# Ones in the graph table's rows, and residuals added by ScalarE and TensorE in the second attention layer of a four-layer graph network

## The chip, the core and the metric

The kernel runs on one core of a Trainium2 chip. The metric is the device time of one execution in microseconds (us): before the change 3109.28 us, the median of four runs that lie between 3100.89 and 3118.96 us. Engines are named as in the profile: PE (TensorE matmuls), PEld (TensorE weight loads), DVE (VectorE), ACT (ScalarE), POOL (GpSimd), SP (SyncE, which here only starts transfers).

## What is computed

Eight batches of 2048 nodes with 128 features pass through four layers on one sparse adjacency matrix. Layers 0 and 2 are attention layers, layers 1 and 3 are graph-attention layers ("graph layers" below). Per batch:

```python
# layers 0 and 2
scores = einsum('bnhd,bmhd->bhnm', x @ Wq, x @ Wk) / sqrt(16), masked by adj     # 8 heads of 16
x = layer_norm(x + (softmax(scores) @ (x @ Wv)) @ Wo + bo) * ln1_g + ln1_b
x = layer_norm(x + relu(x @ W1 + b1) @ W2 + b2) * ln2_g + ln2_b                  # W1: 128x256
# layers 1 and 3
h = x @ W;  e = leaky_relu((h @ a_src)[:, None] + (h @ a_dst)[None, :]), masked by adj
x = layer_norm(x + softmax(e) @ h) * ln_gamma + ln_beta
```

Each node has about 17 neighbours, so the kernel works on lists of neighbours, not on the whole matrix. If a list does not fit, a second, dense program (class `Dense`) runs instead; the given input does not need it.

## The kernel before, in words

**Units and tiles.** The 2048 nodes are cut into 32 units of 64 nodes. A unit holds its nodes for two halves of the batch (4 batches each), so a tile `[128, 512]` is 4 batches of 128 features. The neighbours of a unit are gathered in 9 slots of 128 rows: four pairs and a single one, which makes five steps `t` per unit.

**Tables.** Each layer reads a table in HBM with one row per node. An attention row holds keys and values of all 8 batches, 8 x 256 floats = 8192 bytes. A graph row holds, per batch, the 128 centred features of `h` and one float, the score `h @ a_dst`: 8 x 129 floats = 4128 bytes. `project` (L1290) makes the rows of the next layer from a finished unit (matmul with `Wkv` or `Wx`, copy to `trows`, store L1354 by SP). A layer's gathers (`gather`, L1410, issued by POOL at L1422) wait until the whole table is stored, so between layers the pipeline runs empty and fills again.

**An attention unit** (`attention`, L1437). Queries are made by PE (L1456) and copied by ACT (L1460). Per step: POOL gathers a pair of slots into one of six `kv` buffers; PE spreads the queries over the slots into the four PSUM banks of `qe` (L1495); DVE multiplies keys by them (L1507) and sums over 16 features (L1514); ACT takes the exponent (L1524); POOL, or for some tiles DVE, multiplies values by it (L1533); PE adds the slots up into `acc` and `sums` (L1561), which frees the buffer.

`after_attention` (L1575) then finishes the unit: DVE inverts the sums and divides (L1579 to L1586); PE transposes, ACT copies to `at` (L1606); PE multiplies by `Wo` as one 128x512 matmul into `ps_o` (L1282); DVE adds bias and residual into `r` (`add_to`, L1598); PE multiplies `r` by a constant matrix (identity minus 1/128), which transposes it back and takes the mean away (`centred`, L1272); ACT squares, takes the root and scales (`norm`, L1369 to L1391); PE transposes, ACT applies gain and offset (`scaled`, L1408). Then `W1` with relu (L1282, L1617), `W2` into `ps_y` (L1629), and `add_to`, `centred`, `norm`, `scaled` once more.

**A graph unit** (`graph`, L1649). Per step DVE adds the two scores and applies the leaky slope (L1735, L1742), ACT takes the exponent (L1747), DVE spreads it over a one-hot matrix into `w` (L1757), and PE adds the weighted rows up (L1784): 16 matmuls with 32 columns of weights and 128 features each, all into one PSUM bank, which a matmul with zeros has cleared (L1701). Four more small matmuls per step sum the weights themselves into `sums` (L1795). `after_graph` (L1806) inverts the sums (L1814), scales (L1822), and goes on as above.

**What sets the order.** All operations are recorded first, each with its engine, a cost in microseconds, a key (due time), and the buffers that it takes. `Plan.order` runs a list scheduler over them: on each engine the ready operation with the smallest key goes first, if its buffers are free. The resulting order is fixed in the program, and each engine works through its own list strictly in that order. A changed cost or a changed operation can therefore move operations on all engines, in other layers too. [...]

Of the kernel before, what the change touches and what calls it, by code (L numbers as in the profile page):

```python
# [9 lines left out]
F32 = mybir.dt.float32  # L10
# [730 lines left out]
class Sparse:  # L741
# [15 lines left out]
    def __init__(self, ctx, tc, x, xt, adj, w, out):  # L757
# [16 lines left out]
        for tag, bufs in PSUM_BUFS.items():  # L774
# [14 lines left out]
            self.dram.tile([self.N, self.B * (2 * P if kind is MHA else P + 1)], F32, name=f"table_{n}")  # L789
# [141 lines left out]
    def mha_weights(self, n):  # L931
        const, w = self.const, self.w[n]
        d = {}
        for name, shape in (("Wq", [P, P]), ("Wkv", [P, 2 * P]), ("Wo", [P, P]), ("W1", [P, FFN])):
            if n or name != "Wkv":
                d[name] = const.tile(shape, F32, name=f"{name}_{n}")
        d["W2"] = const.tile([P, FFN // P, P], F32, name=f"W2_{n}")
        if n:
            self.fill(n, (d["Wkv"][:, 0:P], w["Wk"]), (d["Wkv"][:, P : 2 * P], w["Wv"]))
        else:  # L940
            d["Wkv"] = self.layers[0]["Wkv"]
        self.fill(
            n,
            (d["Wq"], w["Wq"]),
            (d["Wo"], w["Wo"]),
            (d["W1"], w["W1"]),
            (d["W2"], w["W2"].rearrange("(c p) m -> p c m", p=P)),
        )
        d["b1"] = self.column(n, "b1", FFN // P)
        for name in ("bo", "ln1_g", "ln1_b", "b2", "ln2_g", "ln2_b"):  # L950
            d[name] = self.column(n, name)
        return d

    def gat_weights(self, n):
# [7 lines left out]
            (wx[:, 0:P], w["W"]),  # L962
# [7 lines left out]
        op({"PE": 0.3}, lambda e: e.transpose(ps.tile[:, 0:P], wx[:, 0:P], self.ident), key, reads=[at], writes=[ps])  # L970
# [10 lines left out]
        def centre(e):  # L981
            e.tensor_copy(wx[:, P : P + 2], ps2.tile[:, 0:2])
            e.tensor_reduce(mean, wx[:, 0:P], axis=mybir.AxisListType.X, op=ALU.add)
            e.tensor_scalar(mean, mean, 1.0 / P, None, ALU.mult)
            e.tensor_scalar(wx[:, 0:P], wx[:, 0:P], mean, None, ALU.subtract)
# [290 lines left out]

    def product(self, w, x, key, name, out):
# [12 lines left out]
    def project(self, n, u, x, key, of=None, shares=()):  # L1290
# [4 lines left out]
        width = 2 * P if mha else P + 1  # L1295
        rows = self.cell(("trows", "hidden", "trows")[u % 3] if n == 0 else "trows", [P, hb * width], name="trows")
        for v in range(2):
# [29 lines left out]
            else:  # L1327

                self.op(
                    {"ACT": 0.48},  # L1330
                    lambda e, ps=ps, v=v: e.copy(
                        rows.tile.rearrange("p (b d) -> p b d", b=hb)[:, 2 * v : 2 * v + 2, :],
                        ps.tile[:, :, 0 : P + 1],
                    ),
# [68 lines left out]
    def scaled(self, rows, gamma, beta, tag, key):  # L1403
# [8 lines left out]
        )  # L1412
        return x
# [158 lines left out]
    def after_attention(self, n, u, acc, sums, x, base):  # L1572
# [34 lines left out]
        r = cell("r", [P, CH], name="r1")  # L1607
        ps = self.product(L["Wo"], at, key, "ps_o", r)
        add_to(r, ps, L["bo"], x, key - 2)
        normed = self.norm(self.centred(r, key), key)  # L1610
        x1 = self.scaled(normed, L["ln1_g"], L["ln1_b"], "x1", key)
# [12 lines left out]
        r = cell("r", [P, CH], name="r2")  # L1624
        ps = cell("m", [P, CH], name="ps_y")
        for f in range(FFN // P):
            op(
                {"PE": 1.0},
                lambda e, f=f, ps=ps: e.matmul(  # L1629
                    ps.tile,  # L1630
                    lhsT=L["W2"][:, f, :],
                    rhs=hidden.tile[:, f, :],
                    start=(f == 0),
                    stop=(f == FFN // P - 1),
                ),
                key,
                reads=[hidden],
                writes=[ps],
                holds=[r],
            )  # L1640
        add_to(r, ps, L["b2"], x1, key - 2)
        normed = self.norm(self.centred(r, key), key)
# [6 lines left out]
    def graph(self, n):  # L1649
        hb = self.HB  # L1650
        width = hb * (P + 1)
        op, cell = self.op, self.cell
        for u in range(self.NU):
# [36 lines left out]
            if u % 2:  # L1690
                both = cell("q", [P, 4, CH], name="acc_q")
                outs = [both]
                acc, sums = (lambda both=both: both.tile[:, 0, :]), (lambda both=both: both.tile[:, 1, 0:hb])
            else:
                outs = [cell("acc", [P, CH]), cell("sums", [P, hb])]
                acc, sums = (lambda outs=outs: outs[0].tile), (lambda outs=outs: outs[1].tile)

            def clear(e, acc=acc):
                for s in range(P // GROUP):
                    rows = slice(s * GROUP, (s + 1) * GROUP)  # L1700
                    e.matmul(  # L1701
                        acc()[rows, :],
                        lhsT=self.zeros[:, 0:GROUP],
                        rhs=self.zeros,
                        start=True,
                        stop=False,
                    )


            op({"PE": 0.3}, clear, base, reads=[te, self.table[n]], writes=outs)  # L1710
# [3 lines left out]
            for i, t in enumerate(steps):  # L1714
# [15 lines left out]
                def both_rows(kv, at=at, tiles=tiles):  # L1730
                    rows = kv.tile[:, at % 4 * 2 * width : (at % 4 + tiles) * 2 * width]
                    return rows.rearrange("p (j b d) -> p j b d", j=tiles, d=P + 1)

                def score(e, t=t, kv=kv, te=te, e8=e8, both_rows=both_rows, tiles=tiles):
# [3 lines left out]
                        both_rows(kv)[:, :, :, P].rearrange("p j (h b) -> p j h b", h=2),  # L1738
# [27 lines left out]
                def add(  # L1766
                    e,
                    t=t,
                    kv=kv,
                    hot=hot,  # L1770
                    e8=e8,
                    w=w,
                    acc=acc,
                    sums=sums,
                    both_rows=both_rows,
                    tiles=tiles,
                    first=i == 0,
                    last=i == TG - 1,
                ):
                    for b in range(hb):  # L1780
                        for j in range(2):
                            for hf in range(2):
                                rows = slice((2 * hf + j) * GROUP, (2 * hf + j + 1) * GROUP)
                                e.matmul(  # L1784
                                    acc()[rows, b * P : (b + 1) * P],
                                    lhsT=w.tile[:, j, hf * hb + b, :],
                                    rhs=both_rows(kv)[:, j % tiles, hf * hb + b, 0:P],
                                    start=False,
                                    stop=(last and b == hb - 1),
                                )  # L1790
                    for j in range(2):
                        for hf in range(2):
                            rows = slice((2 * hf + j) * GROUP, (2 * hf + j + 1) * GROUP)
                            col = GS + (j * TG + t) * GROUP
                            e.matmul(  # L1795
                                sums()[rows, :],
                                lhsT=hot.tile[:, col : col + GROUP],
                                rhs=e8.tile[:, j % tiles, hf * hb : (hf + 1) * hb],
                                start=first,
                                stop=last,  # L1800
                            )

                op({"PE": 1.8}, add, key, reads=[now, hot, e8, w], writes=outs, shares=[kv])
            self.after_graph(n, u, outs, acc, sums, x, base)

    def after_graph(self, n, u, outs, acc, sums, x, base):  # L1806
# [6 lines left out]
        def inverse(e):  # L1813
            e.tensor_scalar(rc.tile, sums(), 1e-30, None, ALU.max)  # L1814
            e.reciprocal(rc.tile, rc.tile)

        op({"DVE": 0.35}, inverse, base, reads=outs, writes=[rc])
        a = cell("rows", [P, hb, P], name="a")
        for b in range(hb):
# [3 lines left out]
                    a.tile[:, b, :], acc()[:, b * P : (b + 1) * P], AF.Copy, scale=rc.tile[:, b : b + 1]  # L1823
# [137 lines left out]
```

## Time and profile before

| | us |
|---|---|
| median of four runs | 3109.28 (3100.89 to 3118.96) |
| the execution that was profiled | 3117.2 |
| span of its profile | 3115.2 |
| layer 0, attention, with the building of the lists | about 0 to 1160 |
| layer 1, graph | about 1200 to 1660 |
| layer 2, attention | about 1670 to 2640 |
| layer 3, graph | about 2643 to 3115 |

Busy time in the span: PE 2435.7 us (78%), PEld 1495.3 (48%), DVE 2210.2 (71%), ACT 1382.4 (44%), POOL 2132.2 (68%). The transfers moved 1087.97 MB.

How to read it. In a group's row stand line, engine, operation, out<-in, the count, then busy time and mean length of one instruction (ns), then the idle time of that engine just before them and what ended it. A matmul of 32-bit floats is two instructions in these counts. In a list of waits, "DVE r L1598 <- PE ps_o L1282" means that DVE stood idle until that PE instruction was done. A table of windows gives for each stretch the busy time and count of PE, PEld, DVE, ACT and POOL, then the granted clock of PE (1.00 is full), the mean busy share of the 16 DMA engines (packets overlap a little, so it can pass 1.00) and the rate. PE's busy time counts pipelined matmuls in full, so the distance from one start to the next tells more. A line of the timeline is start, length, engine, line, operation.

### The profile page before, as it was taken

Reading aid. Unit: us, or ns where it says so; the run is one execution under the profiler, and the core shown is the slowest. Engines: PE = TensorE matmul, PEld = TensorE weight load, DVE = VectorE, ACT = ScalarE, POOL = GpSimd, SP = SyncE. Lnnn points to the kernel's source line nnn. Section 1 sums busy time; section 2 is a strip of 40 time slices with the busy share of each in tenths; the row PEclk is TensorE's granted clock in tenths of the full one; section 3 lists DMA queues with packets and bytes.
Section 4 is the critical chain, followed back from the end, with each engine's and each line's share of the span. In section 5 each row is a group of like instructions: output and inputs, shape, how many; then the busy total and the mean of one; then the engine's idle time right before and its main releaser. Section 6 shows DMA issues by size and latency. Waiting matters only on the chain.

```text
span 3115.2 us, 68763 instructions
## 1 busy us (share of the span) xinstructions
PE 2435.7 (78%) x26280; PEld 1495.3 (48%) x26280; DVE 2210.2 (71%) x3420; ACT 1382.4 (44%) x4749; POOL 2132.2 (68%) x1461
## 2 busy tenths in 40 slices
PE   7878887778877776878887678888888887777775
PEld 5634444344333334767765234333334343666765
DVE  4879998889887772444443888988899894555554
ACT  4535545445544443444444144444444444343433
POOL 1168877768888874656653788888788883766663
PEclk8679989989999997888888799999999998787787
DMA  8889989889998976999997999999899994999996
GB/s 282 291 310 368 370 318 367 318 304 371 363 364 321 356 274 231 411 405 403 398 401 280 369 365 370 369 380 378 342 366 384 375 379 147 388 407 400 400 404 242
DMA packets 270865, 1087.97 MB, mean 349 GB/s; under 512 B 41216, under 2 KB 59904, under 8 KB 198624
## 3 DMA queue, kind: packets, MB, share of 16 engines
q0 software_dynamic: 166848, 866.63, 71.3%
q1 hardware_dynamic: 103680, 216.85, 19.1%
q8 instruction: 211, 3.46, 0.4%
q14 instruction: 126, 1.03, 0.1%
HBM read 1031.29 MB, written 99.75 MB: 363 GB/s over the span
## 4 chain that ended last, share of the span: by engine, by line
DMA 34%; PE 19%; DVE 15%; issue 12%; POOL 9%; ACT 3%; POOLq 0%; DVEq 0%; SPq 0%; ACTq 0%
DMA kv<-table,idx 33%; DVE kv L1507 8%; POOL kv L1533 5%; POOL kv L1422 5%; PE qe L1495 4%; DVE s L1514 3%; PE acc L1561 3%; PE ps_c L1272 2%; PE ps_y L1629 2%; PE acc L1784 1%; PE ps_t L1260 1%; DVE kv L1533 1%; PE ps_f L1282 1%; ACT junk L1369 1%; PE ps_o L1282 1%
## 5 line engine op out<-in xcount | busy, mean ns | idle before, releaser
L1422 POOL DMA_INDIRECT kv<-table,idx x1152 | 1174.9, 1020 | 738.3 <-issue 261.6
L1533 POOL TENSOR_TENSOR kv<-kv 128x2048 f32<-128x2048 f32 (+1 forms) x264 | 944.4, 3589 | 79.0 <-ACT kv L1524 75.2
L1507 DVE TENSOR_TENSOR kv<-qe,kv 128x2048 f32<-128x2048 f32 (+1 forms) x320 | 662.9, 2071 | 168.2 <-DMA kv<-table,idx 136.6
L1514 DVE TENSOR_REDUCE s<-kv 128x128 f32<-128x2048 f32 (+1 forms) x320 | 660.0, 2063 | 7.2
L1495 PE MATMUL qe<-q_sb,hot 32*128 32x512 f32 (+1 forms) x2304 | 397.2, 691 | 189.8 <-DVE kv L1507 188.9
L1561 PE MATMUL acc<-kv,hot 128*32 128x512 f32 x2560 | 361.8, 642 | 40.7 <-POOL kv L1533 29.7
L1784 PE MATMUL acc<-kv,w 128*32 128x128 f32 x5120 | 220.3, 325 | 99.7 <-DVE w L1757 98.2
L1524 ACT ACTIVATE kv<-s 128x128 f32<-128x128 f32 (+1 forms) x320 | 95.1, 297 | 439.3 <-DVE s L1514 312.8
L1757 DVE TENSOR_TENSOR w<-hot,e 128x512 f32<-128x512 f32 (+1 forms) x384 | 221.6, 600 | 72.1 <-ACT e L1747 62.5
L1735 DVE TENSOR_TENSOR e<-te,kv 128x16 f32<-128x16 f32 (+1 forms) x320 | 58.5, 183 | 293.3 <-DMA kv<-table,idx 279.7
L1495 PEld LDWEIGHTS qe<-q_sb,hot 32*128 32x128 f32 (+1 forms) x2304 | 105.9, 195 | 320.8 <-DVE kv L1507 273.8
L1784 PE MATMUL acc_q<-kv,w 128*32 128x128 f32 x5120 | 211.9, 311 | 51.8 <-DVE w L1757 51.1
L1369 ACT ACTIVATE junk<-ps_c,eps 128x128 f32<-128x128 f32 x512 | 187.1, 365 | 125.4 <-PE ps_c L1272 116.3
L1747 ACT ACTIVATE e<-e 128x16 f32<-128x16 f32 (+1 forms) x320 | 67.1, 212 | 372.1 <-DVE e L1742 338.0
L1784 PEld LDWEIGHTS acc<-kv,w 128*32 128x32 f32 x5120 | 164.8, 130 | 130.3 <-DVE w L1757 109.9
L1784 PEld LDWEIGHTS acc_q<-kv,w 128*32 128x32 f32 x5120 | 160.7, 125 | 80.2 <-DVE w L1757 64.3
L1561 PEld LDWEIGHTS sums<-kv,hot 128*32 128x32 f32 x2560 | 87.5, 115 | 209.2 <-issue 204.3
L1282 PE MATMUL ps_f<-x,W 128*128 128x512 f32 x256 | 153.0, 686 | 17.2 <-ACT hidden L1617 6.1
L1272 PE MATMUL ps_c<-centre,r 128*128 128x128 f32 x1024 | 151.5, 293 | 17.0 <-DVE kv L1533 7.6
L1391 ACT ACTIVATE normed<-ps_c,rstd 128x128 f32<-128x128 f32 x512 | 162.2, 365 | 2.5
L1272 PEld LDWEIGHTS ps_c<-centre,r 128*128 128x128 f32 x1024 | 130.5, 199 | 67.3 <-DVE r L1598 25.1
L1260 PE MATMUL ps_t<-ident,normed 128*128 128x128 f32 x640 | 123.5, 311 | 49.3 <-ACT normed L1391 22.1
(154 smaller groups left out, 3786.4 us busy)
## 6 DMA issues: line engine op xcount, KB each, us to landing
hot<-hots SPq DMA_DIRECT2D x128, 480.0 KB
table<-trows SPq DMA_DIRECT2D x128, 256.0 KB
xd<-xnew SPq DMA_DIRECT2D x96, 256.0 KB
x<-xd SPq DMA_DIRECT2D x96, 256.0 KB
kv<-table,idx POOLq DMA_INDIRECT x1152
table<-trows SPq DMA_DIRECT2D x128, 129.0 KB
kv<-adj_dram SPq DMA_DIRECT2D x16, 1024.0 KB
hots<-hot SPq DMA_DIRECT2D x20, 480.0 KB
```

The source lines that it names most:

```text
L1272: e.matmul(ps.tile[:, cols], lhsT=flat(x.tile)[:, cols], rhs=self.centre, start=True, stop=True)
L1282: lambda e: e.matmul(ps.tile, lhsT=w, rhs=x.tile, start=True, stop=True),
L1369: e.activation(self.junk, flat(r.tile)[:, b * P : (b + 1) * P], AF.Square, bias=self.eps, scale=P**-0.5, accum_out=var.tile[:, b : b + 1],)
L1391: lambda e, b=b: e.activation(normed.tile[:, b, :], flat(r.tile)[:, b * P : (b + 1) * P], AF.Copy, scale=rstd.tile[:, b : b + 1],),
L1422: e.indirect_dma_start(out=rows(kv.tile, j), out_offset=None, in_=self.tables[n], in_offset=bass.IndirectOffsetOnAxis(ap=self.idx[:, u, co ...
L1495: e.matmul(qe.tile[:, j, hf, :], lhsT=hot.tile[rows, t * P : (t + 1) * P], rhs=q.tile[rows, :], start=True, stop=True,)
L1507: e.tensor_tensor(k, qe.tile[:, 0:tiles].rearrange("p j h c -> p (j h) c"), k, ALU.mult)
L1514: e.tensor_reduce(s.tile[:, 0 : tiles * heads].rearrange("p (q c) -> p q c", q=2 * tiles), k, axis=mybir.AxisListType.X, op=ALU.add,)
L1533: e.tensor_tensor(v, v, w.unsqueeze(3).to_broadcast([P, 2 * tiles, heads // 2, HD]), ALU.mult)
L1561: e.matmul(out[rows, :], lhsT=hot.tile[:, col : col + GROUP], rhs=rhs[:, 2 * (j % tiles) + hf, :], start=(t == 0), stop=(t == TG - 1),)
L1757: e.tensor_tensor(w.tile[:, j : j + tiles], oh[:, j : j + tiles].unsqueeze(2).to_broadcast(shape), e8.tile[:, 0:tiles].unsqueeze(3).to_bro ...
L1784: e.matmul(acc()[rows, b * P : (b + 1) * P], lhsT=w.tile[:, j, hf * hb + b, :], rhs=both_rows(kv)[:, j % tiles, hf * hb + b, 0:P], start=F ...
```

## The change

1. **Graph rows** become 130 floats per batch (4160 bytes): the score moves to column 0, the features to columns 1 to 128, and column 129 is the constant 1, copied in by ACT. The weighted sum over columns 1 to 129 then gives the features and, in its last column, the sum of the weights. The four sums matmuls per step (L1795) and the clearing matmuls (L1701) go; the result of four batches now takes two PSUM banks of two batches each, in place of one bank and a small tile of sums.
2. **In layer 2 only** (`if n:`), the DVE additions (L1598) go. ACT makes `r = x + bo` from SBUF ahead of time; PE adds `r` times the centring matrix and `at` times `Wo` in one PSUM bank, with the roles of the operands exchanged so that the result is transposed at once (`summed`). For the second half ACT reads the same transposed bank twice: once for `x1`, once for `r = x1 + b2`. The means of the rows of `Wo` and `W2` are taken away once by DVE (`centre_weights`), so that the sum in the bank is centred. Layer 0 keeps the old form.

```diff
-            self.dram.tile([self.N, self.B * (2 * P if kind is MHA else P + 1)], F32, name=f"table_{n}")
+            self.dram.tile([self.N, self.B * (2 * P if kind is MHA else P + 2)], F32, name=f"table_{n}")
...
+    def centre_weights(self, e, n, d):
+
+        mean = self.const.tile([P, 1], F32, name=f"mean_{n}")
+        for w in (d["Wo"], *(d["W2"][:, f, :] for f in range(FFN // P))):
+            e.tensor_reduce(mean, w, axis=mybir.AxisListType.X, op=ALU.add)
+            e.tensor_scalar(mean, mean, 1.0 / P, None, ALU.mult)
+            e.tensor_scalar(w, w, mean, None, ALU.subtract)
+
+        e.tensor_tensor(d["ln1_b2"], d["ln1_b"], d["b2"], ALU.add)
...
+    def summed(self, key, *parts):
+
+        ps = self.cell("m", [P, CH], name="ps_s")
+
+        def term(e, of, w, first, last):
+            for b in range(self.HB):
+                cols = slice(b * P, (b + 1) * P)
+                e.matmul(
+                    ps.tile[:, cols],
+                    lhsT=of()[:, cols],
+                    rhs=w,
+                    start=first and b == 0,
+                    stop=last,
+                    skip_group_check=True,
+                )
...
+                def fill(e, ps=ps, v=v):
+                    row = rows.tile.rearrange("p (b d) -> p b d", b=hb)
+                    e.copy(row[:, 2 * v : 2 * v + 2, 0 : P + 1], ps.tile[:, :, 0 : P + 1])
+                    if v:
+                        e.copy(row[:, :, P + 1], self.ones[:, 0:hb])
...
+        if other:
+            self.op(
+                {"ACT": 0.8},
+                lambda e: e.activation(other.tile, ps.tile, AF.Identity, bias=other_beta, scale=gamma),
...
+            ps = self.summed(key, (r, lambda r=r: r.tile, self.centre), (at, lambda: at.tile, L["Wo"]))
...
+            x1 = self.scaled(normed, L["ln1_g"], L["ln1_b"], "x1", key, r, L["ln1_b2"])
...
+            ps = self.summed(
                 key,
+                (r, lambda: r.tile, self.centre),
+                *((hidden, lambda f=f: hidden.tile[:, f, :], L["W2"][:, f, :]) for f in range(FFN // P)),
+            )
...
-            op({"PE": 0.3}, clear, base, reads=[te, self.table[n]], writes=outs)
...
                                 e.matmul(
-                                    acc()[rows, b * P : (b + 1) * P],
+                                    acc(b)[rows, :],
                                     lhsT=w.tile[:, j, hf * hb + b, :],
-                                    rhs=both_rows(kv)[:, j % tiles, hf * hb + b, 0:P],
-                                    start=False,
-                                    stop=(last and b == hb - 1),
+                                    rhs=both_rows(kv)[:, j % tiles, hf * hb + b, 1 : P + 2],
+                                    start=first and b % 2 == 0,
+                                    stop=last,
+                                    skip_group_check=True,
                                 )
-                    for j in range(2):
-                        for hf in range(2):
-                            rows = slice((2 * hf + j) * GROUP, (2 * hf + j + 1) * GROUP)
-                            col = GS + (j * TG + t) * GROUP
-                            e.matmul(
-                                sums()[rows, :],
-                                lhsT=hot.tile[:, col : col + GROUP],
-                                rhs=e8.tile[:, j % tiles, hf * hb : (hf + 1) * hb],
-                                start=first,
-                                stop=last,
-                            )
-
-                op({"PE": 1.8}, add, key, reads=[now, hot, e8, w], writes=outs, shares=[kv])
+                op({"PE": 1.5}, add, key, reads=[now, w], writes=outs, shares=[kv])
```

In the built programs, from before to after: PE loses 128x512 products (32 of `ps_o`, 64 of `ps_y`), 256 centring matmuls, 1280 sums matmuls and 256 clearing matmuls, and gets 640 matmuls 128x128 of `ps_s`; the 5120 matmuls of the graph layers are 129 columns wide in place of 128. DVE loses 64 additions 128x512 and gets 64 small operations of the inverse and 10 for the weights. ACT gets 64 operations 128x512 and 64 copies 128x4. POOL and SP keep their counts, with rows of 4160 bytes.

## The prediction

> **What bounds the kernel now.** First the page's slices and a table of windows, to see which stage has which limit. The page's DMA line, 40 slices:
>
> ```profile
> DMA  8889989889998976999997999999899994999996
> GB/s 282 291 310 368 370 318 367 318 304 371 363 364 321 356 274 231 411 405 403 398 401 280 369 365 370 369 380 378 342 366 384 375 379 147 388 407 400 400 404 242
> ```
>
> Transfers are near their limit in most slices, with holes where a layer ends (slices 15-16, 22, 34, 40). The windows (busy us of PE, PEld, DVE, ACT, POOL; clock; DMA share; rate), for layer 1, layer 2, two good slices of layer 2, and layer 3:
>
> ```profile
> 1240.00:1640.00 400.00, 328.66 (x6184) 279.50 (x6186) 171.45 (x606) 194.60 (x688) 241.45 (x240) 0.86 1.02 404
> 1750.00:2560.00 810.00, 675.14 (x4966) 314.18 (x4962) 720.28 (x534) 357.33 (x1208) 670.04 (x375) 0.95 0.95 369
> 2028.00:2106.00 78.00, 64.79 (x485) 29.74 (x486) 69.93 (x54) 34.27 (x115) 65.27 (x36) 0.98 0.98 379
> 2340.00:2418.00 78.00, 65.97 (x491) 31.00 (x492) 71.27 (x51) 37.00 (x128) 65.86 (x39) 0.98 0.98 384
> 2650.00:3050.00 400.00, 296.53 (x6299) 266.77 (x6303) 219.22 (x708) 156.25 (x644) 275.29 (x263) 0.77 1.03 400
> ```
>
> The graph layers (first and last row) are held by transfers: share 1.02 and 1.03, no other engine full. In layer 2 the share is 0.95, DVE is busy 720 of 810 us (89%), POOL 670; POOL also loses 63.1 us to the gaps between its gathers (next fence, "issue"), so 733 (90%). Three limits lie within a few per cent of each other. Who waits there, DVE and POOL, in the window 1750 to 2560 (us, times, longest):
>
> ```profile
> DVE kv L1507 <- DMA kv<-table,idx: 42.5, 34, 3.5
> DVE kv L1533 <- ACT ps_e L1524: 22.2, 13, 4.4
> DVE r L1598 <- PE ps_o L1282: 10.7, 6, 2.4
> ...
> POOL kv L1422 <- issue: 63.1, 180, 5.0
> POOL kv L1422 <- PE sums L1561: 30.8, 17, 4.5
> POOL kv L1533 <- ACT kv L1524: 21.2, 11, 3.8
> ```
>
> DVE waits for rows, POOL for a free buffer: a ring in which no engine is the only bound. The 147 multiplications in the window are 29.4 units, so a unit takes 27.55 us; 32 units make the scale 32/29.4 = 1.09.
>
> **The DVE additions of layer 2.** What goes, from the groups of that window:
>
> ```profile
> L1598 DVE SCALAR_TENSOR_TENSOR r<-ps_o,bo,x 128x512 f32<-128x512 f32 x29 | 21.6, 744 | 10.7 <-PE ps_o L1282 10.7
> ...
> L1598 DVE SCALAR_TENSOR_TENSOR r<-ps_y,b,x 128x512 f32<-128x512 f32 x28 | 20.8, 742 | 0.0
> ```
>
> Of 64 additions at 0.743 us, 47.6 us of DVE go; with the wait ahead of them (10.7 x 1.09 = 11.7) at most 59 us, if DVE alone set the pace. From below: nothing, if rows and POOL set it. From the transfers' side: with the share up from 0.95 to the graph layers' 1.02, 810 x (1 - 0.95/1.02) x 1.09 = 61 us; to the 0.98 of the two good slices, 810 x (1 - 0.95/0.98) x 1.09 = 27 us. I take 27: it is what this same mix of 8 KB rows, POOL and DVE reaches when it runs well, and lies near the middle of 0 and 59. What is late next is the gather, then POOL, whose 733/29.4 = 24.9 us per unit are untouched (DVE falls from 24.5 to 23.0).
>
> **What takes their place.** ACT: per unit one pass over `x` in SBUF and one more over the bank of `ps_t`. Nearest rows: the copy L1460 at 584 ns, the scaled pass L1408 at 776. So 1.2 to 1.6 us per unit, 37 to 50 us in layer 2. ACT is busy 357 of 810 us there, so the cover is its 56% of idle time; if an exponent has to stand behind them, see the third rival. PE, start to next start in the timeline: a 128x512 product about 1.0 us, four centring matmuls 1.09 (2019.47 to 2020.56). Before: three products and two centrings, 5.2 us; after: five groups like centring, 5.45. I take +0.25 us per unit, at nothing: PE no longer stops for DVE between product and centring (in the window, PE's waits behind `r` were a few us), and PE is not last in the waits above. The second reader keeps a bank of `m` 0.8 us longer, but two of about 13 banks per unit fall away; at nothing, bounded by one such pass (0.78 x 32 = 25 us) either way; the listing of the changed order shows the `qe` spreads as regularly placed as before. `x` is read by ACT rather than DVE; SP's next load of `x`, which waited for DVE's addition, waits for ACT; it is loaded well ahead, at nothing.
>
> **The weights' means, once.** Ten small DVE operations; from the graph weights' rows (reduce 277, scale 154, subtract 287 ns) 3 x 0.72 + 0.17 = 2.3 us. The listing puts them behind the last but one addition of layer 0. There, SP's last weight transfer starts at 1177.10, and DVE stands idle from 1176 on:
>
> ```profile
> 1175.23 0.75 DVE L1598 SCALAR_TENSOR_TENSOR r<-ps_y,b,x 128x512 f32<-128x512 f32 x1 [5.62 <-PE ps_y L1629]
> 1187.98 0.75 DVE L1598 SCALAR_TENSOR_TENSOR r<-ps_y,b,x 128x512 f32<-128x512 f32 x1 [12.01 <-PE ps_y L1629]
> ```
>
> Landing some 4 us after the start (the last table store before the gathers: 2639.41 to 2643.13) plus 2.3 us ends by 1184: hidden with 4 us to spare. Behind this new wait stand the last addition and `t` (L1342). If the landing takes as long as the slowest load of a `hot` tile on the chain of waits (11.8 us), the end of layer 0 moves by 3 to 4 us.
>
> **The passage from layer 2 to 3.** POOL stands still until the last unit's rows are stored:
>
> ```profile
> 2611.01 2.05 PE L1282 MATMUL ps_o<-at,Wo 128*128 128x512 f32 x2
> 2613.09 0.75 DVE L1598 SCALAR_TENSOR_TENSOR r<-ps_o,bo,x 128x512 f32<-128x512 f32 x1 [2.23 <-PE ps_o L1282]
> 2614.55 1.26 PE L1272 MATMUL ps_c<-centre,r 128*128 128x128 f32 x8
> 2615.85 0.37 ACT L1369 ACTIVATE junk<-ps_c,eps 128x128 f32<-128x128 f32 x1 [0.36 <-PE ps_c L1272]
> ...
> 2643.13 1.02 POOL L1422 DMA_INDIRECT kv<-table,idx  x1 [43.21 <-DMA table<-trows]
> ```
>
> From product to first square 4.8 us here and 4.1 (2627.11 to 2631.21) in the second half; two or three groups of 1.09 to 1.8 us (slow clock) replace each. Gain between 0 and 5, taken as 3. The copy of ones in `project` (like the 128x4 logarithm, 206 ns) adds 0.2 us at two passages: +0.4.
>
> **The graph layers.** The sums (0.15 to 0.22 us per step, start to start) and the clearing (0.3 to 0.6 per unit) go from PE; the inverse takes one more DVE operation (157 ns), and a matmul of 129 columns one part in 128 more of its 47 ns spacing. All this lies under the transfers and counts nothing; it would count if PE set the pace. The rows grow by 32/4128 = 0.78%. Rows are 263/9 = 29.2 units x 9 x 128 x 4128 bytes = 139 of the 160 MB that the last window moved, 87%. So 800 us x 0.87 x 0.78% = +5.4 us. Below: 0, if time goes by rows and not by bytes; a gain has no row for it. I take +5.
>
> [...]
>
> **The sum** against the profiled execution: 3117.2 - 27 - 3 + 0.4 + 5 = 3092.6. That execution lies 7.9 us above the median of the four runs, so I forecast 3085.
>
> **Rivals.** *DVE was the pace (17%):* rows do arrive when asked sooner, and layer 2 gives the whole 59. For it: DVE's 89%, and 24.5 us per unit; against: it waits 42.5 us for rows. 3117.2 - 59 - 3 + 0.4 + 5 = 3060.6, by the median 3053. *Rows and POOL were (18%):* the freed DVE time turns into more waiting for rows, 0 in place of 27: 3119.6, by the median 3112. For it: POOL's 90% is not touched. That the rearranged order of the whole program, layer 0 included, eats what DVE saves would end here too. *ACT's new passes stand in front of the exponents (19%):* POOL's multiplication starts from ACT's exponent and already waits 21.2 us for it. ACT works in order, and if per unit one of the five exponents comes behind a pass of 0.78 us on top, POOL's buffers come free later: 32 x 0.78 = +25 us, where POOL has no slack to give: its 27.55 - 24.9 = 2.6 us per unit are already waits of which exponents and buffers, 30.8 + 21.2 us over 29.4 units, make 1.8. It decides once the exponents' waits grow by more than DVE's gain shortens the ring. 3117.2 + 25 + 2.4 = 3144.6, by the median 3137.
>
> **How the numbers follow.** The forecast has 46%, its own range 3068 to 3100. Measurements of this kernel can tell about 0.5% (15.5 us) from no change, so faster is below 3094. Of the 46, 7 lie in 3094 to 3100. Faster: 39 + 17 = 56%; same: 7 + 18 = 25%; slower: 19%. The range 3046 to 3128 takes in the fast rival with 6 us under it and half of the way to the slow one (about 12% above, 5% below are left out).
>
> **What would show it.** In layer 2 of the changed profile: DMA share 0.97 to 0.99, about 26.7 us per unit, DVE waiting longer for rows, and no addition of L1598 left to wait for. Graph windows: share still 1.02, their length +0.6%, PE busy down by a tenth or more. Passage to layer 3: POOL's wait about 40 us. Wrong if ACT's exponents (L1524) become the waits of POOL, if layer 2's share stays at 0.95, or if layer 0 moves by over 5 us.

## The result, and the profile after

The changed kernel takes 3119.73 us (median of 52 runs, 3098.75 to 3137.45), the kernel before 3108.53 (78 runs, 3090.83 to 3128.82): ratio 1.0031, 95% interval 1.002 to 1.0041. The forecast was 3085, in a range of 3046 to 3128. The change costs some 10 us where a gain was expected; of the rivals, the one in which the freed DVE time is worth nothing (3112) lies nearest.

One profile each does not show this: the profiled executions have 3108.8 us (after, 10.9 below its median) and 3117.2 (before, 8.7 above). So the stages are compared below over several profiles. The page of the changed kernel, its DMA lines in 40 slices:

```profile
DMA  8889998999998949999997999999889984999996
GB/s 275 282 328 390 366 334 341 376 357 382 368 363 332 350 166 346 412 407 405 398 409 281 361 379 363 378 372 385 339 337 358 369 317 149 395 406 406 402 400 249
```

The graph layers (slices 17 to 21 and 35 to 39) stand near 400 GB/s as before; layer 2 (slices 23 to 33) has three 8s where it had one. The table of windows of the same kernel, for the same three windows as in the prediction (busy us of PE, PEld, DVE, ACT, POOL; clock; DMA share; rate):

```profile
1240.00:1640.00 400.00, 312.45 (x5019) 248.03 (x5021) 177.33 (x634) 190.90 (x689) 242.74 (x241) 0.83 1.02 407
1750.00:2560.00 810.00, 662.43 (x5334) 363.67 (x5330) 665.45 (x463) 392.67 (x1284) 652.41 (x363) 0.94 0.93 362
2650.00:3050.00 400.00, 288.13 (x5113) 238.40 (x5114) 224.10 (x744) 157.14 (x648) 275.10 (x263) 0.77 1.02 403
```

DVE's busy time in layer 2 fell, 720 to 665 us, as the additions went. But the DMA share fell too, 0.95 to 0.93, where 0.97 to 0.99 was forecast, and POOL did less in the same time (652 for 670). Who waits in that window, after:

```profile
DVE kv L1567 <- DMA kv<-table,idx: 49.7, 33, 4.4
DVE kv L1593 <- ACT ps_e L1584: 27.2, 17, 7.0
DVE kv L1567 <- PE qe L1555: 26.7, 15, 4.1
DVE rc L1639 <- PE sums L1621: 15.8, 4, 6.9
DVE t L1394 <- PE ps_p L1356: 9.5, 9, 2.0
...
POOL kv L1482 <- issue: 60.8, 169, 5.5
POOL kv L1593 <- ACT kv L1584: 39.4, 17, 5.8
POOL kv L1482 <- PE sums L1621: 28.3, 19, 4.9
```

DVE now waits 26.7 us for `qe` and 15.8 for the sums, 3.1 and 2.3 in the whole of layer 2 before:

```profile
DVE kv L1507 <- PE qe L1495: 3.1, 9, 0.8
DVE rc L1579 <- PE sums L1561: 2.3, 2, 1.8
```

POOL waits 39.4 us for exponents, 21.2 before. A stage runs from the first gather of its layer (the one that waits for the table) to the next. The whole of layer 2, before and then after:

```profile
1712.31:2643.13 930.82, 755.68 (x5444) 352.29 (x5444) 787.96 (x592) 399.35 (x1350) 729.65 (x409) 0.93 0.91 352
```

```profile
1681.75:2635.53 953.78, 756.38 (x6012) 413.07 (x6012) 749.17 (x528) 444.11 (x1446) 730.08 (x409) 0.92 0.89 344
```

Layer 2 is 23 us longer with 39 us less of DVE's work. The other stages: layer 0 1201.4 and 1173.5 us (in another execution of the changed kernel, e12, it took 1202.2), layer 1 510.9 and 508.3, layer 3 472.1 and 471.6.

### The profile page after: what moved, and what is told of

Same layout as the page of the kernel before. It is cut to its first block, busy times and chain, and to the rows that moved or that the text cites. A ratio compares the mean times of both kernels' runs of the same rounds, so it can differ in the third digit from the quotient of the medians.

```text
span 3107.1 us, 64257 instructions
## 1 busy us (share of the span) xinstructions
PE 2389.3 (77%) x24040; PEld 1475.3 (47%) x24040; DVE 2180.7 (70%) x3432; ACT 1426.8 (46%) x4877; POOL 2133.8 (69%) x1461
## 5 line engine op out<-in xcount | busy, mean ns | idle before, releaser
L1621 PE MATMUL acc<-kv,hot 128*32 128x512 f32 x2560 | 368.6, 654 | 56.2 <-POOL kv L1593 49.5
L1846 PE MATMUL acc<-kv,w 128*32 128x129 f32 x2560 | 143.0, 352 | 164.1 <-DVE w L1831 141.1
L1846 PE MATMUL acc_q<-kv,w 128*32 128x129 f32 x5120 | 204.1, 304 | 73.5 <-DVE w L1831 68.2
L1846 PEld LDWEIGHTS acc<-kv,w 128*32 128x32 f32 x2560 | 82.5, 135 | 210.2 <-DVE w L1831 169.8
L1421 ACT ACTIVATE junk<-r,eps 128x128 f32<-128x128 f32 x256 | 102.4, 400 | 101.5 <-DVE r L1887 96.2
L1621 PEld LDWEIGHTS acc<-kv,hot 128*32 128x32 f32 x2560 | 52.9, 112 | 200.1 <-issue 96.9
L1693 ACT ACTIVATE hidden<-ps_f,b 128x512 f32<-128x512 f32 x128 | 87.5, 685 | 122.4 <-PE ps_f L1331 122.0
L1846 PE MATMUL sums<-kv,w 128*32 128x129 f32 x2560 | 136.1, 340 | 0.0
L1281 PE MATMUL ps_t<-ident,normed 128*128 128x128 f32 x640 | 116.3, 311 | 22.1 <-ACT normed L1443 8.5
```

Of the source, the lines that this page charges most:

```text
L1281: e.transpose(ps.tile[:, b * P : (b + 1) * P], flat(x.tile)[:, b * P : (b + 1) * P], self.ident)
L1421: e.activation(self.junk, flat(r.tile)[:, b * P : (b + 1) * P], AF.Square, bias=self.eps, scale=P**-0.5, accum_out=var.tile[:, b : b + 1],)
L1621: e.matmul(out[rows, :], lhsT=hot.tile[:, col : col + GROUP], rhs=rhs[:, 2 * (j % tiles) + hf, :], start=(t == 0), stop=(t == TG - 1),)
L1846: e.matmul(acc(b)[rows, :], lhsT=w.tile[:, j, hf * hb + b, :], rhs=both_rows(kv)[:, j % tiles, hf * hb + b, 1 : P + 2], start=first and b ...
```

## The experiments

The chips differ. On those of e1 to e12, e17 and e18 the kernel before takes 3350 to 3373 us, since the graph layers take longer there (in e9, layer 1 612.7 us and layer 3 600.8); on that of e13 to e16 it takes 3104.51. Layer 2 with the work and order of before takes 922.9 to 938.3 us over four profiles, and layer 0 lies within what it varies between executions. So totals are compared by their ratio to the kernel before on the same chip, stages by profile.

The expectations weigh these theories: O, later L (the new fixed order of layer 2 makes the engines wait), R (rows and POOL's ring set the pace and DVE's time is free), A (ACT's new passes delay the exponents), B (the two rotating PSUM banks of the pool `m`, which in layer 2 takes all PSUM results but `qe`, `acc` and `sums`), P (TensorE's work on the sums), G (the graph part).

**The two parts alone: e1, e2, e16.** e1 and e16 are the changed kernel with `if n:` turned to `if False:` in `mha_weights` and `after_attention`, so that layer 2 does the work of before; e2 is the kernel before with those parts of the diff.

> The graph-layer part of the change alone (rows with a 1, no sums and no clearing on TensorE); layer 2 as before. Theory O (the loss comes from the new fixed order of layer 2): what is changed here lies under the transfers, so the time stays within 8 us of before (3100 to 3117), with a DMA share of 1.02 in the graph stages. Theory G (the graph part itself costs): rows longer by 0.78% lengthen two stages of about 500 us by up to 5 us each, 3114 to 3120, and the graph windows move the same number of rows in more time. Either way the order of the whole list is another one than before, so a move of layer 2 or 0 here, with their work unchanged, is the size of what the order alone can do.

> The layer-2 part of the change alone; graph rows and sums as before. Theory O: the loss of the changed kernel (+11 us) is here, 3112 to 3130, layer 2 longer than before with more waits of VectorE behind TensorE. Theory G: no slower than before, 3085 to 3109, since the graph part is what costs.

> The graph-layer part of the change alone, as e1, beside e14 on the same chip. Layer 2 in the order of before, 930 to 942; if the graph stages are slow on this chip (600 us and more for the last), the last one is 20 to 30 us shorter than in the kernel before and the ratio 0.988 to 0.994; if they are fast (472 us), 0.994 to 1.0. It should beat e14 unless e14's layer 2 falls under 935.

e1: 0.991 of before (0.9884 to 0.9936). e16: 0.9916 (0.9887 to 0.9945). e2: 1.0129 (1.0094 to 1.0164). On the chip of e16 the graph part gains 26 us (0.84% of 3104.51); on that of e1 and e2 it gains 0.9%, and the layer-2 part loses 1.3%. The product of these two, 1.0038, is near the result's 1.0031, but in part by luck: e2 runs layer 2 in an order of its own and takes 970.1 us there, 39 more than e1, where the changed kernel takes 23 more than the kernel before; and e1's gain stands in a layer 3 that is slow on its chip (586.2 us, 614.2 in e3). On such a chip the whole change is about even: e12 took 3347.59 us in its one run, the kernel before 3349.89. Theory G falls, and so does the "within 8 us" of theory O for e1.

**Less work in an unchanged order: e3, e4, e8.** The order of instructions on every engine stays, only columns or matmuls are left out:

```diff
# e3, on before, with cut = 32 in layer 2
-e.scalar_tensor_tensor(r.tile, ps.tile, bias, other.tile, ALU.add, ALU.add)
+e.scalar_tensor_tensor(r.tile[:, 0:cut], ps.tile[:, 0:cut], bias, other.tile[:, 0:cut], ALU.add, ALU.add)
# e4, on after: both new activations on [:, 0:32], the first matmuls of a sum on one column
# e8, on after, in summed
-for b in range(self.HB):
+for b in range(1 if first else self.HB):
```

> The kernel before with its order of instructions unchanged on every engine, but VectorE's 64 additions of layer 2 work on 32 of their 512 columns, and the centring matmuls read one column 128 times over: most of the residual sums is left out. About 42 us of VectorE's work go and nothing takes its place. Theory O (relief of VectorE is worth something, the new order ate it): 20 to 40 us faster, 3070 to 3090, VectorE waits longer for rows. Theory R (rows and GpSimd's ring set the pace of layer 2, VectorE's time is free): within 8 us of before, 3100 to 3116, with VectorE's waits for rows and exponents grown by about what was taken away.

> The changed kernel with its order of instructions unchanged on every engine, but ScalarE's two new passes of layer 2 work on 32 of their 512 columns, and the first matmul group of each sum reads one column 128 times over: most of the residual sums is left out. About 35 to 40 us of ScalarE's work go. Theory A (the new passes stand in front of the exponents and GpSimd waits): 15 to 25 us faster than the changed kernel, 3095 to 3105. Theories O and R: within 8 us of the changed kernel, 3112 to 3127.

> The changed kernel with its order of instructions unchanged on every engine, but the first group of each sum has one matmul in place of four (three quarters of the residual are left out): TensorE loses some 0.8 us of work twice per unit, about 52 us in layer 2, and each sum's bank is held 0.8 us less. Theory P (TensorE's work is what grew): layer 2 falls by 25 to 50 us, to 905 to 930. Theory B: by about 64 x 0.8 us of bank time over two banks, at most 25 us: 930 to 945. Theory L (the order itself makes the engines wait): within 8 us of 954.

e3: 1.0002 of before (0.998 to 1.0024). A small addition still takes 0.244 us, so 64 x (0.744 - 0.244) = 32 us of DVE's work went, not 42; layer 2 took 921.3 us, some 10 less than 931, and DVE's wait for rows stayed where it was (64.7 before, 60.8 now).

```profile
L1603 DVE SCALAR_TENSOR_TENSOR r<-ps_o,bo,x 128x32 f32<-128x32 f32 x32 | 7.8, 245 | 10.6 <-PE ps_o L1285 10.6
1822.26:2743.60 921.34, 743.83 (x5444) 348.91 (x5444) 759.22 (x592) 399.31 (x1350) 729.39 (x409) 0.94 0.92 356
```

Theory R's time holds, though the longer waits for rows that it named did not come: in this order DVE's work is worth a third of itself at most. e4: layer 2 955.0 us against 953.8 in the changed kernel, with the two passes at 371 and 315 ns in place of 771 and 715; theory A falls. e8: 967.3 us, no less than 968.6 and 969.6 in e7 and e5 on the same chip, though PE was busy 736 us and not 761; theory P gets nothing from it. But e5 and e7 have other orders, the whole change in the order of e8 was not profiled on that chip, and the granted clock in layer 2 is 0.90 there, 0.92 in the changed kernel's profile.

**The banks: e5, e6.** e5 reads the finished tile instead of the bank, e6 also takes DVE's exponents from SBUF:

```diff
# e5, in scaled (other_beta is then b2)
-lambda e: e.activation(other.tile, ps.tile, AF.Identity, bias=other_beta, scale=gamma),
+lambda e: e.activation(other.tile, x.tile, AF.Identity, bias=other_beta),
# e6: the second exponent (into ps_e) goes
-lambda e, kv=kv, ps=ps, weigh=weigh: weigh(e, kv, ps.tile),
+lambda e, kv=kv, weigh=weigh: weigh(e, kv),
```

> The changed kernel, but ScalarE's second new pass makes its residual from the finished tile in SBUF (x1 plus b2) and no longer from the PSUM bank of ps_t: the same number of passes, the bank comes free one pass earlier, 32 times. The list scheduler makes another order of it. Layer 2 measured so far: 931 and 931 us in two kernels with the work and order of before, 921 with small additions, 954 and 955 in the changed order, 970 with the same work in another order. Theory B (the two rotating PSUM banks, which the sums now hold for 10 us at a time, set the pace of each unit's tail): layer 2 falls to 930 to 945. Theory P (TensorE's longer work on the sums): 950 to 958. Theory L (only the accident of the order): anything from 935 to 970. If layer 2 stands at 940, the whole kernel is 4 to 8 us faster than before on a chip with fast graph stages.

> As e5, and the 40 weighings on VectorE take their exponents from SBUF, where ScalarE writes them anyway, so that no PSUM bank is held for them (about 3 us each, 117 to 126 us per layer 2 in the traces). Theory B: layer 2 falls by another 10 to 20 us, to 915 to 930. Theory P: no change from e5 but for 40 exponents less, 945 to 955. It fails in its own way if VectorE with both operands in SBUF holds GpSimd up: GpSimd's weighing (3.58 us each) would then show longer instructions.

e5: 0.9984 (0.9956 to 1.0012), layer 2 969.6 us. e6: 1.0142 (1.0112 to 1.0171), layer 2 993.1. What theory B forecast came in neither. But each has an order of its own, and e10 below shows what an order alone can cost, so the banks are not ruled out; e6 says little besides: DVE and POOL got in each other's way, as was named, but on DVE's side. e6's groups of DVE's weighing, then those of e5, which has `ps_e` in PSUM (both over the whole program):

```profile
L1593 DVE TENSOR_TENSOR kv<-kv 128x1024 f32<-128x1024 f32 x48 | 147.6, 3074 | 11.6 <-ACT kv L1584 10.6 <-ACT normed L1443 1.0
L1593 DVE TENSOR_TENSOR kv<-kv 128x2048 f32<-128x2048 f32 x8 | 30.6, 3829 | 0.4 <-ACT kv L1584 0.4
```

```profile
L1593 DVE TENSOR_TENSOR kv<-kv,ps_e 128x1024 f32<-128x1024 f32 x48 | 58.2, 1213 | 27.1 <-ACT ps_e L1584 27.1
L1593 DVE TENSOR_TENSOR kv<-kv,ps_e 128x2048 f32<-128x2048 f32 x8 | 18.2, 2277 | 0.0
```

**The same work in another order: e7, e9, e10, e12.** In the kernel before, the order in layer 2 repeats itself every four units; in the changed kernel it does not. GpSimd's order of eight or nine units (G a gather of two tiles, g of one, W a weighing), cut for the eye in the first by its period:

```
before  WGWGWGGgWGGWWWGGgWGWGWGGWWgGWGWGGgW | WGWGWGGgWGGWWWGGgWGWGWGGWWgGWGWGGgW | WGWGWGG
after   GWGWGGgWGWWGWGGgWGWGWWGGWgGWGWWGGWgGWGWGGgGWWGWWGGgGWWGWGGWWgGWGGWWGgWGWGGGWgGWWGG
```

e7 and e10 change one number that the scheduler books, and no instruction:

```diff
# e7, on after, in summed
-{"PE": 1.1},
+{"PE": 1.2},
# e10, on before, in add_to
-{"DVE": 0.72},
+{"DVE": 0.69 if n else 0.72},
```

> The changed kernel with one number of the scheduler's changed: a term of a sum is booked with 1.2 us in place of 1.1. The work is the same in every instruction, only the order differs. Theory L (order): layer 2 moves by over 8 us from 954, to either side. Theories B and P: within 8 us of 954.

> The kernel before as it is, for its stage lengths on the chip on which the next three run. All theories: layer 2 at 930 to 942, and the lengths of the other stages are the measure for those of the next three.

> The kernel before with one number of the scheduler's changed: an addition of layer 2 is booked with 0.69 us in place of 0.72. The work is the same in every instruction; only the order differs. In the order of before, the engines' sequences in layer 2 repeat every four units (96% of GpSimd's steps, 95% of VectorE's, 94% of TensorE's are the same as the step one period earlier); with 0.69 they don't (47, 25 and 16%), as they don't in the changed kernel (51, 45 and 25%). Theory L (the lost period is what costs): layer 2 is 12 to 30 us longer than in the kernel before on the same chip, the ratio 1.004 to 1.009. Theories B and P (the sums' longer hold of the banks, or TensorE's work): within 6 us, ratio 0.998 to 1.002.

> The changed kernel as it is, for its stage lengths on the same chip. All theories: layer 2 some 20 to 35 us longer than in the kernel before on this chip, layer 0 shorter by 5 to 20 us.

Layer 2: e9 938.3 us, e10 961.9, e12 959.6, all on one chip; e7 968.6 on another. e10's ratio is 1.0075 (1.0045 to 1.0106). So the kernel before, with every instruction the same, loses 23.6 us by another order, one without a period: as much as the change does. That the lost period is what costs, and not something else in that order, is not shown. The waits of POOL in layer 2, e9 and then e10:

```profile
POOL kv L1533 <- ACT kv L1524: 24.4, 15, 2.7
POOL kv L1422 <- PE sums L1561: 24.0, 11, 4.6
```

```profile
POOL kv L1533 <- ACT kv L1524: 45.8, 20, 7.5
POOL kv L1422 <- PE sums L1561: 25.5, 17, 4.4
```

The wait for exponents nearly doubles without any new pass on ACT: in the changed kernel, too, it can be a sign of the order. e12's layer 0 (1202.2 us) was not shorter than e9's (1197.5), against what was expected.

**The changed work in regular orders: e11, e14, e15, e13.** Again one number or key each; e13 is e11 with e8's edit.

```diff
# e11, in attention
-op({"PE": 1.5}, add, key, reads=[kv, hot], writes=[acc, sums])
+op({"PE": 1.575 if n else 1.5}, add, key, reads=[kv, hot], writes=[acc, sums])
# e14, in gather
-{"POOL": 1.3 * tiles},
+{"POOL": (1.261 if n == 2 else 1.3) * tiles},
# e15, in attention
-op({"PE": 1.2}, spread, key - 6, reads=[q, hot], writes=[qe])
+op({"PE": 1.2}, spread, key - (10 if n else 6), reads=[q, hot], writes=[qe])
```

> The changed kernel with one number of the scheduler's changed: in layer 2 an accumulation on TensorE is booked with 1.575 us in place of 1.5. The work is the same in every instruction, and the order becomes regular: 97, 97 and 95% of the steps of GpSimd, VectorE and TensorE repeat after four units. Theory L: layer 2 falls by 20 to 45 us against the changed kernel on the same chip, to what it is in the kernel before or up to 15 us under it, and the whole beats both. Theories B and P: within 8 us of the changed kernel.

> The kernel of e11 (the changed work in a regular order) with that order unchanged on every engine, but the first group of each sum has one matmul in place of four (three quarters of the residual are left out): about 52 us less of TensorE's work in layer 2. Theory P (in a regular order it is TensorE's longer work on the sums that keeps layer 2 over that of before): layer 2 falls from 953 by 10 us or more, to 930 to 943. Theory L (it is how this order stands to the real times): within 6 us of 953.

> The changed kernel in another regular order: in layer 2 a gather is booked with 1.261 us per tile in place of 1.3 (94, 92 and 85% of the steps of GpSimd, VectorE and TensorE repeat after four units). The work is the same. Theory L: regular orders differ among each other too; layer 2 between 925 and 950, on one side of e11's 953. Theory P: within 6 us of e11's 953, since TensorE's work is the same.

> The changed kernel in a third regular order: the spreads of the queries on TensorE get an earlier key in layer 2 (ten in place of six ahead; 96, 97 and 94% of the steps repeat). The work is the same. Theory L: layer 2 between 925 and 960, not the same as e11 and e14. Theory P: within 6 us of 953.

e11: 0.9937 (0.9912 to 0.9962), layer 2 952.8 us; e14: 1.0049 (1.0028 to 1.007), 955.7; e15: 958.9; e13: 943.8. Theory L falls short: three regular orders of the changed work are hardly shorter than the irregular one (953.8, 959.6; on one chip e11 is 7 us under e12, where 20 to 45 were forecast), and on one chip e14 lies 33 us above the 922.9 of e16, which has the work and order of before. e14 and e15 lie within 6 us of 953, as theory P said. (e11 as a whole still beats the kernel before: layer 3, slow on its chip, took 577.3 us, 600.8 in e9.) e13 lies between the two forecasts (against e11 on another chip, 9 us for 36 us less of PE's busy time): not decided. The whole of layer 2 in e16 and e14, and who waits there:

```profile
1702.08:2624.98 922.90, 750.34 (x5436) 349.49 (x5436) 787.36 (x592) 402.56 (x1382) 729.59 (x408) 0.94 0.91 356
```

```profile
DVE kv L1567 <- DMA kv<-table,idx: 55.7, 34, 18.6
DVE t L1394 <- PE ps_p L1356: 9.3, 5, 4.7
```

```profile
1695.90:2651.57 955.67, 751.85 (x6012) 416.50 (x6012) 748.23 (x528) 439.99 (x1446) 730.26 (x408) 0.93 0.88 343
```

```profile
DVE kv L1567 <- DMA kv<-table,idx: 113.9, 64, 19.1
DVE t L1394 <- PE ps_p L1356: 39.8, 16, 20.8
```

DVE has 39 us less to do in e14 and waits 58 us longer for rows. (Of the 39.8 us behind `ps_p`, 30.5 lie at the end of the layer, where DVE has no additions left between its last instructions.)

**Halves: e17, e18.** One of the two sums of a unit is put back to what it was:

```diff
# e17, in after_attention, the second and third "if n:"; e18 the first
-if n:
+if False:
# e17, the products with W2, for a regular order
-{"PE": 1.0},
+{"PE": 0.95 if n else 1.0},
# e18, the reduction, for a regular order
-op({"DVE": 1.12 * tiles}, reduce, key, reads=[kv], writes=[s])
+op({"DVE": (1.0864 if n else 1.12) * tiles}, reduce, key, reads=[kv], writes=[s])
```

> The changed kernel with only the first of the two sums of layer 2 (x plus bias by ScalarE, Wo and centring in one bank); the second half of a unit as before, with VectorE's addition. One number of the scheduler's makes the order regular (a product with W2 booked with 0.95 us; 96, 97 and 94% of the steps repeat). The graph part alone measured 0.991 and 0.992 of before, the whole change 1.003. Theory 1 (the loss comes with the first sum: ScalarE's early pass holds one of two buffers of r from before the attention is divided): 1.001 to 1.006, layer 2 at 945 to 960. Theory 2 (it comes with the second sum, whose bank stays open over three groups): 0.990 to 0.996, layer 2 at 922 to 940. Theory E (each adds its share): 0.996 to 1.001.

> The changed kernel with only the second of the two sums of layer 2 (ScalarE's second pass over the bank of ps_t, W2 and centring in one bank); the first half of a unit as before, with VectorE's addition. One number of the scheduler's makes the order regular (VectorE's reduction booked with 1.086 us per tile; 92, 92 and 89% of the steps repeat). Theory 1: 0.990 to 0.996, layer 2 at 922 to 940. Theory 2: 1.001 to 1.006, layer 2 at 945 to 960. Theory E: 0.996 to 1.001.

e17: 0.9949 (0.9924 to 0.9973), layer 2 942.9 us. e18: 0.9964 (0.994 to 0.9987), 954.0. Against e1 and e16 the first sum adds about 0.4% and the second 0.5%, which would be theory E. But e17 lies under its window, the intervals overlap, and e11, with both sums, stands at 0.9937, under either half: the orders differ by as much as the halves, and which sum costs is not decided.

## Why the prediction was wrong

The prediction said that layer 2 is "a ring in which no engine is the only bound", and then priced the additions by shares of busy time. The trace has a direct measure of that ring. Each of the 160 steps holds one of six `kv` buffers from its gather to its accumulation, so one microsecond of hold per step is worth 160/6 = 26.7 us of layer 2. The means over all 160 steps, from the starts and ends of the trace's rows (us; up to the accumulation's start, which itself takes 1.2 us more in each of these):

| kernel | gather to multiplication | to the sum's end | to the exponent's end | to the accumulation | hold | layer 2 |
|---|---|---|---|---|---|---|
| before | 14.03 | 4.58 | 0.49 | 10.74 | 29.84 | 930.8 |
| e9 (before) | 13.88 | 4.61 | 0.50 | 10.83 | 29.82 | 938.3 |
| e16 (work of before) | 13.81 | 4.58 | 0.47 | 10.69 | 29.55 | 922.9 |
| e10 (before, irregular) | 14.14 | 4.56 | 0.71 | 11.37 | 30.78 | 961.9 |
| after | 15.04 | 4.41 | 0.51 | 10.68 | 30.64 | 953.8 |
| e12 (after) | 14.99 | 4.41 | 0.61 | 10.72 | 30.73 | 959.6 |
| e11 (after, regular) | 12.85 | 4.48 | 0.62 | 12.60 | 30.55 | 952.8 |
| e14 (after, regular) | 12.83 | 4.48 | 0.64 | 12.69 | 30.64 | 955.7 |

The differences fit within some 5 us: after against before 0.80 x 26.7 = 21 us (23 measured), e12 against e9 24 (21), e11 against e9 19 (14), e10 against e9 26 (24), e14 against e16 29 (33). A buffer is held 0.7 to 1.1 us longer. This is bookkeeping: it tells where in a step the time goes, not what puts it there. e17 does not fit it: its steps hold a buffer as long as those of e1 (29.5 us), and its layer 2 is 11.5 us longer.

In the changed order the row waits longer for its multiplication, and not for the transfer: from the landing of a step's rows to its multiplication it is 3.35 us (1.90 before; 3.42 in e12, 2.19 in e9), from the gather to the landing 11.69 (12.13 before). DVE then stands in front of instructions that wait for PE and ACT, as its waits above show. e10 has this too (3.04), with the work of before, so an order alone can bring it. In the regular orders the multiplication comes a microsecond earlier (1.17 us after the landing in e11 and e14; the relief is there), and two are lost behind the exponent: in e14 a weighing by POOL starts 4.36 us after its exponent (2.91 in e16), and the accumulation 4.94 us after the weighing's end (4.20); in e11 it is 4.21 and 4.95, in e9 3.23 and 3.88 (means over all 120 weighings of POOL).

Point by point:

- *The additions, "I take 27": failed.* An addition is in no step's hold; it counted only by what it pushed back. Taken away alone, with the order kept (e3), they gave about 10 us of 32 in layer 2 and a ratio of 1.0002. The bound from below, nothing, was the nearer one, and the share of 0.98 that two good slices reached was not reached by giving DVE less to do: it fell from 0.95 to 0.93.
- *"The listing of the changed order shows the `qe` spreads as regularly placed as before": failed.* The order lost its period of four units, and DVE's wait for `qe` went from 3.1 to 26.7 us. That another order alone can cost as much as the whole loss is shown for the kernel before (e10, 23.6 us). The second rival named the rearranged order, but let it eat only the gain.
- *PE's five groups and the longer use of a bank, "at nothing": open.* PE's busy time in layer 2 is the same (755.7 and 756.4 us). In every order that was tried the changed work takes longer than that of before in its own order, 14 us (e11 to e9) to 36 us (e15 to e16), and three regular orders agree within some 6 us, which speaks for a cost of the work. But the work of before was run in only one other order, and there it took 961.9 us, no less than the changed work on the same chip (959.6 and 952.8). So the share of the work and that of the order are not told apart; a second regular order of the work of before was not run. Which of the new dependences could do it (PE's groups between the accumulations, the bank held over a whole sum, the early hold of an `r` buffer) stays open too. A third bank for `m` was not tried.
- *ACT's passes covered by idle time: right* (e4). The two passes took 47.6 us in layer 2, within the 37 to 50. The third rival's sign appeared, POOL waiting for exponents, but cutting the passes short gave nothing (e4), and another order alone brings it (e10).
- *The weights' means hidden in layer 0: nothing speaks against it.* Five profiles with the layer 0 of before have 1194.0 to 1201.4 us, fourteen with that of the graph part 1173.5 to 1202.2 (without e6, whose weighings differ there too); the means are 1198 and 1188.
- *The passage to layer 3, -3: not in POOL's wait*, which is 43.1 us, 43.2 before. From the end of the last accumulation to the first gather of layer 3 it is 37.0 us and was 39.4, so some 2 us came there and were lost ahead of it.
- *The graph rows, +5: failed, and with it "counts nothing".* The windows show 407 and 403 GB/s for 404 and 400, and layer 3 is no longer (471.6 for 472.1): rows 0.78% longer, with the sums and the clearing gone from PE in the same stage, cost nothing that can be seen; the two were not run apart. PE's busy time in these windows fell by 5 and 3%, not by the tenth that was named. The part as a whole gains 26 us on the chip of e16. Part of that is layer 0 in its other order (about 10 us by the means above); e16's profiled execution, 18 us above its median, does not show the rest. Where layer 3 is slow, the gain stands there: 600.8 us in e9, 572.5 in e12. POOL's waits in that layer, e9 and then e12:

```profile
POOL kv L1422 <- PE acc_q L1795: 74.3, 20, 11.2
...
POOL kv L1422 <- PE sums L1795: 50.8, 17, 6.7
...
POOL kv L1422 <- PE acc_q L1784: 39.9, 13, 7.6
POOL kv L1422 <- PE acc L1784: 19.7, 10, 3.0
```

```profile
POOL kv L1482 <- PE acc_q L1846: 87.4, 30, 7.4
...
POOL kv L1482 <- PE sums L1846: 57.2, 26, 4.5
```

There buffers wait for PE's accumulations, 185 us before and 145 after, and the stage is 28 us shorter: on such a chip taking the sums and the clearing from PE pays, it seems.

The step that failed first is thus the 27 us for the additions: with the order kept, they were worth about 10. What turned a small gain into a loss of 23 to 33 us in layer 2 is the new order, the new work, or both. The best version is the graph part alone, 0.991 and 0.9916 of before.

## What to carry to other kernels

Where a ring of buffers sets the pace, price an edit by the time that a buffer is held, step by step from the trace, and not by the busy share of an engine: work outside the hold was worth a third of itself here. With a list scheduler, run the old work in another order too before a loss is put down to the new work: one booked number changed by 0.03 us cost 0.75% here. Try the parts of a change alone before they are joined: a gain of 0.9% was hidden under a larger loss.

## What the runs showed of the hardware

DVE's weighing of 128x1024 took 3074 ns on average with both operands in SBUF (e6), 1213 with one in PSUM (e5). In e6 the 18 of 48 that met no weighing of POOL took 1211 to 1245 ns. The 29 that began beside one, or had one begin within 0.5 us, took 2332 to 7435 ns, and each ended 1.08 to 1.09 us after the end of the last POOL weighing that it met (the one left had POOL begin after 0.95 us and took 1226). In e5, 23 met one and took 1201 to 1222. POOL's own instructions hardly changed (3690 and 3691 ns for 128x2048). In the 29 of e6 DVE ended only behind POOL; the cause in the hardware is not shown.

The same program ran layer 1 at 404 GB/s in the window 1240 to 1640 on one chip and at 334 on another (e9; the whole layer took 510.9 us and 612.7), with layer 0 (1201.4 and 1197.5 us) and layer 2 (930.8 and 938.3) nearly unchanged. What differs between the chips is not shown by these profiles.
